# Grouping layer 2's half-array products by two head pairs, C's product as one task, one pool of PSUM banks, and the planner's weight at 25

## The chip, the cores and the metric

The kernel runs on one core of one Trainium2 chip. The metric is the device time of the whole program in microseconds. A ratio is the mean time of one kernel's fast runs over that of the other's fast runs of the same rounds on the same chip, with a 95% interval; it is therefore not quite the ratio of the medians quoted beside it. In the views of the profile PE is TensorE, DVE VectorE, ACT ScalarE and POOL GpSimd, and L605 is line 605 of the kernel.

## The reference, cut to what matters

Four graph layers in a row over 64 graphs of 256 nodes and 512 features, all in fp32. Each layer normalises, applies a relu, and adds its result to x. Layer 2 has 8 heads of 64:

```python
Xp = einsum('bnd,hdk->bhnk', X, Wp) + bp
Xc = einsum('bhnk,hjk->bhnj', Xp, C)
attn = tanh(A[:, None] * einsum('bhnj,bhmj->bhnm', Xc, Xp))
Xh = einsum('bhnm,bhmk->bhnk', attn, Xp)
out = relu(moveaxis(Xh, 1, 2).reshape(B, N, -1))
```

Layer 1 is a masked softmax over neighbours (a leaky relu of a sum of two vectors, plus -1e10 where there is no edge, minus the row maximum, exp).

## The kernel before: the parts concerned

A small planner in Python splits every graph into tasks, keeps five graphs in flight, and emits the tasks in the order in which its own table of engine lengths says they can start. Pools of buffers and PSUM banks are part of that plan; `BEHIND` weighs the older graph against the longer rest of work. The build then still reorders single instructions on each engine.

```python
IN_FLIGHT = 5
BEHIND = 20.0
PAIR_BUFS = 4
ACC_BANKS = 4
# ... (cut)
keep("acc", ACC_BANKS, [P, 512], banks)
keep("tr", 8 - ACC_BANKS, [P, 512], banks)
# ... (cut)  layer 2, one head pair p = heads 2p and 2p+1, each on 64 of the 128 rows
def scores(p):
    @task(f"ps{p}", f"xc{p // 2}", [("PE", 1.1), ("V", 1.37), ("A", 0.7)], {f"pair:th{p}": 1},
          {"xpt": (1, HP), "xc": (1, HP), "at": (1, HP)}, banks=2)
    def _(*ps):
        # ... (cut)
        for m in range(NC):
            for s in range(2):
                half = slice(s * U, (s + 1) * U)
                nc.tensor.matmul(ps[s][:, m, :], g["xpt"][half, p, m * P:(m + 1) * P],
                                 g["xc"][half, p, :], start=True, stop=True)                  # L605
        for s in range(2):
            nc.vector.tensor_tensor(th[:, s], ps[s], g["at"], OP.mult)                        # L608
            nc.scalar.activation(th[:, s], th[:, s], AF.Tanh)                                 # L609
```

`spread(p)` (L626) multiplies the tanh of one pair with Xp, the two heads on two halves of the columns; `times_c` (L589) makes Xc, each head on half the rows and half the columns. The tanh results lie in the same four `pair` buffers as layer 1's attention.

```python
# layer 1, per head pair: ScalarE, then GpSimd, then VectorE, then ScalarE
nc.scalar.activation(e[:, s, j, :], g["all:es"][:, h, :], AF.Prelu, ...)                      # L511, four times
nc.gpsimd.tensor_tensor(e, e, g["negt"][:, None].to_broadcast([P, 2, NC, N]), OP.add)         # L513
nc.vector.tensor_tensor(e, e, g["all:m"][...].to_broadcast([P, 2, NC, N]), OP.subtract)       # L519
nc.scalar.activation(e, e, AF.Exp)                                                            # L521
# and, for the row maxima, on VectorE, 16 times per graph
nc.vector.tensor_tensor_reduce(junk, g["all:en"][:, h, :], g["neg"][:, c, :], ..., OP.max, ...)  # L477
```

## Time and profile before

| | before |
|---|---|
| three runs | 4454.2, 4455.4, 4460.2 us |
| TensorE busy | 98% |
| VectorE, ScalarE, GpSimd busy | 62%, 38%, 26% |

The lines of the page and of the timeline that carry this are in the prediction. First the groups of VectorE: line, operation, tiles and shapes, count, then busy time in total and the mean ns of one, then VectorE's idle time before it and what ended it.

TensorE's waits: who waited for whom, us in total, times, longest.

```profile
PE tr L263 <- DMA mask_rows<-in_nodemask_dram: 25.9, 1, 25.9
PE tr L365 <- DVE hn L357: 12.4, 3, 5.6
...
PE acc L626 <- ACT pair L609: 6.1, 6, 2.9
...
PE tr L440 <- DVE ec L431: 3.4, 2, 3.0
```

The first is the wait for the first loads at the start. The rest is small, and it lies in the first 700 and the last 200 us of the span.

### The profile page before, as it was taken

The numbers are of one execution on the slowest core, as the hardware profiler recorded it, in microseconds if no ns is written. First come the engines' busy times: TensorE is split into PE (matmuls) and PEld (weight loads), VectorE is DVE, ScalarE is ACT, GpSimd is POOL, SyncE is SP. The second block draws the span as 40 slices with busy tenths as digits, with TensorE's granted clock in tenths as the row PEclk, the third lists the DMA queues.
The fourth block names the chain that finished last, engine by engine and source line by source line (L and its number), as shares of the span: only waits on it lengthen the run. The fifth ranks groups of instructions, "written<-read, shape, count | busy, mean of one in ns | idle before, by whom it ended". The sixth has DMA issues, their size and how long they took to land.

```text
span 4449.4 us, 60495 instructions
## 1 busy us (share of the span) xinstructions
PE 4357.1 (98%) x22850; PEld 2997.4 (67%) x22850; DVE 2761.2 (62%) x7530; ACT 1679.7 (38%) x3333; POOL 1175.1 (26%) x969
## 2 busy tenths in 40 slices
PE   6899999999999999999999999999999999999998
PEld 4666666666666667667666666667667666666665
DVE  4765666666666665666666666666666666666653
ACT  1343333433433443443343333333334334334332
POOL 1321222322322322322322222222223223223220
PEclk9899999999999999999999999999999999999999
DMA  4212112122122121221221221221221221221210
GB/s 127 97 54 79 63 70 86 56 79 84 58 79 78 64 79 69 74 79 67 75 77 69 76 77 65 80 77 61 75 86 60 75 86 60 76 86 57 79 53 15
DMA packets 125382, 323.67 MB, mean 73 GB/s; under 512 B 19040, under 2 KB 66208, under 8 KB 100512
## 3 DMA queue, kind: packets, MB, share of 16 engines
q1 hardware_dynamic: 109568, 311.99, 19.3%
q10 hardware_dynamic: 15520, 7.80, 0.7%
q8 instruction: 179, 2.93, 0.3%
q14 instruction: 115, 0.94, 0.1%
HBM read 284.62 MB, written 35.13 MB: 72 GB/s over the span
## 4 chain that ended last, share of the span: by engine, by line
PE 89%; DVE 2%; DMA 1%; issue 0%; ACT 0%; POOL 0%; SPq 0%; POOLq 0%; DVEq 0%; ACTq 0%
PE tr L296 21%; PE acc L296 19%; PE tr L655 10%; PE acc L538 9%; PE tr L605 6%; PE acc L626 6%; PE tr L365 5%; PE tr L681 5%; PE tr L589 3%; PE tr L639 1%; PE tr L574 1%; PE tr L408 1%; DVE junk L477 1%; PE tr L335 1%; PE tr L301 1%
## 5 line engine op out<-in xcount | busy, mean ns | idle before, releaser
L296 PE MATMUL acc<-wv_s,ht 128*128 128x512 f32 x2048 | 932.0, 598 | 1.9 <-ACT ht L366 1.9
L513 POOL TENSOR_TENSOR pair<-pair,negt 128x1024 f32<-128x1024 f32 x256 | 606.7, 2371 | 801.8 <-ACT pair L511 777.1
L609 ACT ACTIVATE pair<-pair 128x512 f32<-128x512 f32 x512 | 310.0, 627 | 884.7 <-DVE pair L608 878.1
L296 PEld LDWEIGHTS acc<-wv_s,ht 128*128 128x128 f32 x2048 | 379.8, 191 | 379.4 <-issue 366.6
L549 POOL TENSOR_TENSOR xt<-xt,o 128x256 f32<-128x256 f32 x256 | 184.5, 731 | 1546.3 <-DVE o L547 1529.3
L538 PE MATMUL acc<-feats,pair 128*128 128x65 f32 x4096 | 508.4, 276 | 10.2 <-DVE xt L316 5.6
L538 PEld LDWEIGHTS acc<-feats,pair 128*128 128x128 f32 x4096 | 491.6, 195 | 37.6 <-issue 25.9
L511 ACT ACTIVATE pair<-all,ec 128x256 f32<-128x256 f32 x1024 | 453.2, 499 | 85.9 <-PE acc L626 50.4
L296 PE MATMUL tr<-w_s,ht 128*128 128x512 f32 x1024 | 465.7, 598 | 2.9 <-ACT ht L366 2.6
L655 PE MATMUL tr<-ht,m_s 128*128 128x256 f32 x2048 | 457.1, 382 | 0.0
L346 DVE BATCH_NORM_STATS2 stats<-xt 128x6 f32<-128x512 f32 x512 | 340.4, 679 | 141.7 <-DMA xt<-in_x_dram 140.7
L655 PEld LDWEIGHTS tr<-ht,m_s 128*128 128x128 f32 x2048 | 386.1, 191 | 54.5 <-issue 4.2
L366 ACT ACTIVATE ht<-tr 128x512 f32<-128x512 f32 x512 | 279.7, 596 | 357.5 <-PE tr L365 297.3
L477 DVE CUSTOM_DVE_ANT_0 junk<-all,neg 128x256 f32<-128x256 f32 x1024 | 390.0, 445 | 4.7 <-DMA all<-er_d 4.6
L357 DVE TENSOR_SCALAR hn<-xt,mv,rstd 128x512 f32<-128x512 f32 x512 | 267.8, 555 | 185.7 <-POOL rstd L351 169.8
L608 DVE TENSOR_TENSOR pair<-tr,at 128x512 f32<-128x512 f32 x512 | 329.3, 683 | 64.2 <-PE tr L605 60.7
L605 PE MATMUL tr<-xc,xpt 64*128 64x256 f32 x2048 | 333.3, 406 | 0.4 <-DVE pair L608 0.4
L521 ACT ACTIVATE pair<-pair 128x1024 f32<-128x1024 f32 x256 | 269.4, 1058 | 166.6 <-DVE pair L519 158.2
L626 PE MATMUL acc<-pair,xp 128*64 128x256 f32 x2048 | 322.0, 396 | 6.2 <-ACT pair L609 6.1
L296 PEld LDWEIGHTS tr<-w_s,ht 128*128 128x128 f32 x1024 | 190.4, 192 | 193.7 <-issue 185.4
L351 POOL TENSOR_TENSOR rstd<-rstd,power 128x2 f32<-128x2 f32 x256 | 227.7, 890 | 313.2 <-DVE rstd L350 296.4
L519 DVE TENSOR_TENSOR pair<-pair,all 128x1024 f32<-128x1024 f32 x256 | 302.6, 1222 | 9.9 <-POOL pair L513 6.3
(87 smaller groups left out, 5272.9 us busy)
## 6 DMA issues: line engine op xcount, KB each, us to landing
all<-er_d SPq DMA_DIRECT2D x128, 1024.0 KB, 4.5
all<-m_d SPq DMA_DIRECT2D x64, 1024.0 KB, 4.6
xt<-in_x_dram SPq DMA_DIRECT2D x64, 512.0 KB, 3.6
adj<-in_adj_dram SPq DMA_DIRECT2D x128, 256.0 KB, 2.6
out_dram<-xt SPq DMA_DIRECT2D x64, 512.0 KB, 4.8
mask_in<-in_nodemask_dram SPq DMA_DIRECT2D x64, 128.0 KB, 3.2
w_n<-in_L_gnn_Wqk_dram ACTq DMA_DIRECT2D x16, 128.0 KB, 3.8
wv_s<-in_L_gnn_W_v_dram ACTq DMA_DIRECT2D x1, 1024.0 KB
```

The lines of the kernel that those rows point to most:

```text
L296: nc.tensor.matmul(p, ht[:, k, c * P:(c + 1) * P], w[:, k], start=(k == 0), stop=(k == KC - 1))
L346: nc.vector.bn_stats(stats[:, c, :], xt[:, c, :])
L477: nc.vector.tensor_tensor_reduce(junk, g["all:en"][:, h, :], g["neg"][:, c, :], 1.0, -BIG, OP.add, OP.max, st["mx"][:, c, h:h + 1])
L511: nc.scalar.activation(e[:, s, j, :], g["all:es"][:, h, :], AF.Prelu, bias=st["ec"][:, j, H + h:H + h + 1], alpha=0.2)
L513: nc.gpsimd.tensor_tensor(e, e, g["negt"][:, None].to_broadcast([P, 2, NC, N]), OP.add)
L519: nc.vector.tensor_tensor(e, e, g["all:m"][:, 2 * p:2 * p + 2, None, :].to_broadcast([P, 2, NC, N]), OP.subtract)
L538: nc.tensor.matmul(po[i][:, h % 4, :], e[:, s, j, i * P:(i + 1) * P], feats[:, j, h, :], start=(j == 0), stop=(j == NC - 1))
L605: nc.tensor.matmul(ps[s][:, m, :], g["xpt"][half, p, m * P:(m + 1) * P], g["xc"][half, p, :], start=True, stop=True)
L608: nc.vector.tensor_tensor(th[:, s], ps[s], g["at"], OP.mult)
L609: nc.scalar.activation(th[:, s], th[:, s], AF.Tanh)
L626: nc.tensor.matmul(pyt[s * U:(s + 1) * U, p % 2, :], g["xp"][:, m, h * U:(h + 1) * U], g[f"pair:th{p}"][:, s, m, :], start=(m == 0), stop= ...
L655: nc.tensor.matmul(pz[:, s, :], m3_s[:, k, d * P:(d + 1) * P], g["ht"][:, k, :], start=(k == 0), stop=(k == KC - 1))
```

## The change

Its intent: let the half-array products of layer 2 stand together in longer groups, so that TensorE changes the shape of its array less often. The two pools of banks become one, and the planner's weight `BEHIND` goes from 20 to 25, which also gives a new order to all the rest. The core of the diff, with cuts marked:

```diff
-BEHIND = 20.0
+BEHIND = 25.0
-ACC_BANKS = 4
+PASSING_BANKS = 4
-    keep("acc", ACC_BANKS, [P, 512], banks)
-    keep("tr", 8 - ACC_BANKS, [P, 512], banks)
+    keep("bank", 8, [P, 512], banks)
 ... (cut: a held bank is granted only if four others are free for passing tasks)
-        def times_c(q):
-            @task(f"xc{q}", ..., [("PE", 1.0), ("V", 0.7)], {} if q else {"xc": 1}, banks=2)
-                        nc.tensor.matmul(pc[s][half, r, :], c2_s[half, 2 * q + r, :],
-                nc.vector.tensor_copy(xc[0:U, 2 * q:2 * q + 2, :], pc[0][0:U])
-                nc.scalar.copy(xc[U:P, 2 * q:2 * q + 2, :], pc[1][U:P])
+        @task("xc", "xpt0 xpt1", [("PE", 1.9), ("V", 0.7)], {"xc": 1}, banks=2)
+                        nc.tensor.matmul(pc[q][half, r, :], c2_s[half, 2 * q + r, :],
+            nc.vector.tensor_copy(xc[:, 0:2, :], pc[0])
+            nc.scalar.copy(xc[:, 2:4, :], pc[1])
-        def scores(p):
-            @task(f"ps{p}", ..., [("PE", 1.1), ("V", 1.37), ("A", 0.7)], {f"pair:th{p}": 1}, ..., banks=2)
+        def scores(q):
+            @task(f"ps{q}", ..., [("PE", 1.95), ("V", 2.75), ("A", 0.7)],
+                  {f"pair:th{2 * q}": 1, f"pair:th{2 * q + 1}": 1}, ..., banks=4)
 ... (cut: spread and its output likewise, two pairs in a task)
```

More of the change, by code (lines that the diff above doesn't have):

```diff
@@ L66, in ready @@
         at = max((ends[d] for d in task.after), default=0.0)
-        need = {"tr": task.banks} if task.banks else {}
+        need = {"bank": task.banks} if task.banks else {}
         for kind, n in task.take.items():
             kind = kind.split(":")[0]
+            if kind == "bank":
+                n += PASSING_BANKS
             need[kind] = need.get(kind, 0) + n
@@ L73, in ready @@
                 return None
-            at = max(at, sorted(self.pools[kind])[n - 1][0])
+            at = max(at, sorted(self.pools[kind])[n - 1 - (PASSING_BANKS if kind == "bank" and not task.banks else 0)][0])
         return at
@@ L84, in issue @@
             g.has.setdefault(kind, []).extend(self.grab(kind.split(":")[0]) for _ in range(n))
-        passing = [self.grab("tr") for _ in range(task.banks)]
+        passing = [self.grab("bank") for _ in range(task.banks)]
         task.run(*[t[2] for t in passing])
@@ L106, in issue @@
             g.until[kind] = max(at, g.until.get(kind, 0.0)) if g.users[kind] else 0.0
-        self.pools["tr"] += [(at, i, t) for _, i, t in passing]
+        self.pools["bank"] += [(at, i, t) for _, i, t in passing]
     def run(self, graph, count):
@@ L205, in passing @@
         turn[0] += 1
-        return plan.pools["tr"][turn[0] % (8 - ACC_BANKS)][2]
+        return plan.pools["bank"][4 + turn[0] % 4][2]
     def load_weight(name, src):
@@ L267, in tile_four_gnn_layers @@
     m3_s = consts.tile([P, KC, D], F32)
-    pm3 = [t for _, _, t in plan.pools["acc"]]
+    pm3 = [t for _, _, t in plan.pools["bank"][:4]]
     wqk3_v = wqk3.rearrange("(k p) (s e) -> p k s e", p=P, s=2)
@@ L374, in _ @@
                 @task(f"pv{layer}{c}", f"ht{layer}{c}" + (f" <pv{layer}0" if c else ""), [("PE", 3.47)],
-                      {"acc": 1}, {"ht": (1, users)})
+                      {"bank": 1}, {"ht": (1, users)})
                 def _():
-                    st[f"pv{c}"] = g.has["acc"][-1][2]
+                    st[f"pv{c}"] = g.has["bank"][-1][2]
                     rows(st[f"pv{c}"], g["ht"], c, wv)
@@ L384, in _ @@
                 st["w"] = softmax_nodes(pr, st["wc"])
-            @task(f"add{layer}", f"soft{layer} pv{layer}0 pv{layer}1", [("V", 1.5)], {}, {"acc": NC})
+            @task(f"add{layer}", f"soft{layer} pv{layer}0 pv{layer}1", [("V", 1.5)], {}, {"bank": NC})
             def _():
@@ L526, in gather @@
             if p % 2:
-                give["acc"] = NC
+                give["bank"] = NC
             @task(f"po{p}", f"eb{p} fb0 fb1" + (f" <po{p - 1}" if p else ""), steps,
-                  {} if p % 2 else {"acc": NC}, give)
+                  {} if p % 2 else {"bank": NC}, give)
             def _():
-                po = [t[2][:, :4 * UE].rearrange("p (q u) -> p q u", q=4) for t in g.has["acc"]]
+                po = [t[2][:, :4 * UE].rearrange("p (q u) -> p q u", q=4) for t in g.has["bank"]]
                 e, feats, xt = g[f"pair:e{p}"], g["feats"], g["xt"]
@@ L577, in graph, with _ @@
             turn_xp(c)
-        def times_c(q):
-            @task(f"xc{q}", "xpt0 xpt1" + (" <xc0" if q else ""), [("PE", 1.0), ("V", 0.7)],
-                  {} if q else {"xc": 1}, banks=2)
-            def _(*pc):
-                pc = [t.rearrange("p (a n) -> p a n", a=2) for t in pc]
-                xpt, xc = g["xpt"], g["xc"]
+        @task("xc", "xpt0 xpt1", [("PE", 1.9), ("V", 0.7)], {"xc": 1}, banks=2)
+        def _(*pc):
+            pc = [t.rearrange("p (a n) -> p a n", a=2) for t in pc]
+            xpt, xc = g["xpt"], g["xc"]
+            for q in range(HP // 2):
                 for r in range(2):
@@ L588, in _ @@
                         half = slice(s * U, (s + 1) * U)
-                        nc.tensor.matmul(pc[s][half, r, :], c2_s[half, 2 * q + r, :],
+                        nc.tensor.matmul(pc[q][half, r, :], c2_s[half, 2 * q + r, :],
                                          xpt[half, 2 * q + r, :], start=True, stop=True)
-                nc.vector.tensor_copy(xc[0:U, 2 * q:2 * q + 2, :], pc[0][0:U])
-                nc.scalar.copy(xc[U:P, 2 * q:2 * q + 2, :], pc[1][U:P])
-        for q in range(HP // 2):
-            times_c(q)
@@ L596, in scores @@
-        def scores(p):
-            @task(f"ps{p}", f"xc{p // 2}", [("PE", 1.1), ("V", 1.37), ("A", 0.7)], {f"pair:th{p}": 1},
-                  {"xpt": (1, HP), "xc": (1, HP), "at": (1, HP)}, banks=2)
+            nc.vector.tensor_copy(xc[:, 0:2, :], pc[0])
+            nc.scalar.copy(xc[:, 2:4, :], pc[1])
+        def scores(q):
+            @task(f"ps{q}", "xc" + (f" <ps{q - 1}" if q else ""), [("PE", 1.95), ("V", 2.75), ("A", 0.7)],
+                  {f"pair:th{2 * q}": 1, f"pair:th{2 * q + 1}": 1},
+                  {"xpt": (1, 2), "xc": (1, 2), "at": (1, 2)}, banks=4)
@@ L599, in _ @@
             def _(*ps):
                 ps = [t.rearrange("p (m n) -> p m n", m=NC) for t in ps]
-                th = g[f"pair:th{p}"]
-                for m in range(NC):
-                    for s in range(2):
-                        half = slice(s * U, (s + 1) * U)
-                        nc.tensor.matmul(ps[s][:, m, :], g["xpt"][half, p, m * P:(m + 1) * P],
-                                         g["xc"][half, p, :], start=True, stop=True)
-                for s in range(2):
-                    nc.vector.tensor_tensor(th[:, s], ps[s], g["at"], OP.mult)
-                    nc.scalar.activation(th[:, s], th[:, s], AF.Tanh)
@@ L612, in spread @@
-        def spread(p):
-            take, give = {} if p % 2 else {"acc": 1}, {f"pair:th{p}": 1, "xp": (1, HP)}
-            if p == 0:
-                take["cols"] = 1
-            if p % 2:
-                give["acc"] = 1
-            @task(f"py{p}", f"ps{p}" + (f" <py{p - 1}" if p else ""),
-                  [("PE", 1.1)] + ([("A", 0.6)] if p % 2 else []), take, give)
-            def _():
-                pyt = g["acc"].rearrange("p (r n) -> p r n", r=2)
-                for m in range(NC):
-                    for s in range(2):
-                        h = 2 * p + s
-                        nc.tensor.matmul(pyt[s * U:(s + 1) * U, p % 2, :], g["xp"][:, m, h * U:(h + 1) * U],
-                                         g[f"pair:th{p}"][:, s, m, :], start=(m == 0), stop=(m == NC - 1))
-                if p % 2:
-                    nc.scalar.activation(g["cols"][:, p - 1:p + 1, :], pyt, AF.Relu)
@@ L630, in graph @@
-        for p in range(HP):
-            scores(p)
-        for p in range(HP):
-            spread(p)
+                for r in range(2):
+                    p = 2 * q + r
+                    for m in range(NC):
+                        for s in range(2):
+                            half = slice(s * U, (s + 1) * U)
+                            nc.tensor.matmul(ps[2 * r + s][:, m, :], g["xpt"][half, p, m * P:(m + 1) * P],
+                                             g["xc"][half, p, :], start=True, stop=True)
@@ new lines, in _, with spread @@
+                for r in range(2):
+                    th = g[f"pair:th{2 * q + r}"]
+                    for s in range(2):
+                        nc.vector.tensor_tensor(th[:, s], ps[2 * r + s], g["at"], OP.mult)
+                        nc.scalar.activation(th[:, s], th[:, s], AF.Tanh)
+        def spread(q):
+            take = {"bank": 1} if q else {"bank": 1, "cols": 1}
+            @task(f"py{q}", f"ps{q}" + (f" <py{q - 1}" if q else ""), [("PE", 1.95), ("A", 0.6)], take,
+                  {f"pair:th{2 * q}": 1, f"pair:th{2 * q + 1}": 1, "bank": 1, "xp": (1, 2)})
+            def _():
+                pyt = g["bank"].rearrange("p (r n) -> p r n", r=2)
+                for r in range(2):
+                    p = 2 * q + r
+                    for m in range(NC):
+                        for s in range(2):
+                            h = 2 * p + s
+                            nc.tensor.matmul(pyt[s * U:(s + 1) * U, r, :], g["xp"][:, m, h * U:(h + 1) * U],
+                                             g[f"pair:th{p}"][:, s, m, :], start=(m == 0), stop=(m == NC - 1))
+                nc.scalar.activation(g["cols"][:, 2 * q:2 * q + 2, :], pyt, AF.Relu)
@@ L635, in back @@
+        for q in range(HP // 2):
+            scores(q)
+        for q in range(HP // 2):
+            spread(q)
         def back(c):
-            @task(f"y{c}", "py1 py3", [("PE", 0.5), ("V", 0.69)], {}, {"cols": (1, NC)}, banks=1)
+            @task(f"y{c}", "py0 py1", [("PE", 0.5), ("V", 0.69)], {}, {"cols": (1, NC)}, banks=1)
             def _(py):
```

## The prediction

> **What bounds the kernel now.** I read the page's busy row first, then the chain of work that ended last, then stretches of the span, then the timeline of TensorE alone.
>
> ```profile
> PE 4357.1 (98%) x22850; PEld 2997.4 (67%) x22850; DVE 2761.2 (62%) x7530; ACT 1679.7 (38%) x3333; POOL 1175.1 (26%) x969
> ...
> PE 89%; DVE 2%; DMA 1%; issue 0%; ACT 0%; POOL 0%; SPq 0%; POOLq 0%; DVEq 0%; ACTq 0%
> ...
> 1000.00:2000.00 1000.00, 1000.00 (x5295) 689.74 (x5294) 630.64 (x1745) 389.55 (x775) 273.11 (x223) 1.00 0.21 74
> 2000.00:3000.00 1000.00, 999.88 (x5292) 689.40 (x5292) 630.17 (x1742) 386.70 (x768) 271.45 (x222) 1.00 0.21 74
> ```
>
> TensorE is busy 98% of the span, 89% of the last chain is TensorE, and in the stretches from 1000 to 3000 us it has no idle time at all (the first busy figure after the stretch's length) at a granted clock of 1.00. The next engine, VectorE, has over a third of its time free. So the time is the length of TensorE's stream, and the 92 us in which TensorE is not busy lie at the two ends: 26 us are the first wait for the weights. A microsecond taken out of the stream is a microsecond of time, unless TensorE then waits.
>
> The second question is whether "busy" hides anything, because ends of matmuls are modelled. So I use starts. Every fp32 matmul is two records. In the timeline each row gives start, length, and the number of records:
>
> ```profile
> 2050.44 1.14 PE L605 MATMUL tr<-xc,xpt 64*128 64x256 f32 x8
> 2051.51 1.08 PE L626 MATMUL acc<-pair,xp 128*64 128x256 f32 x8
> 2052.52 1.09 PE L574 MATMUL tr<-ident,xp 128*128 128x128 f32 x8
> 2053.54 1.14 PE L605 MATMUL tr<-xc,xpt 64*128 64x256 f32 x8
> 2054.61 1.09 PE L626 MATMUL acc<-pair,xp 128*64 128x256 f32 x8
> 2055.62 2.00 PE L538 MATMUL acc<-feats,pair 128*128 128x65 f32 x16
> 2057.55 0.65 PE L626 MATMUL acc<-pair,xp 128*64 128x256 f32 x2
> 2058.13 0.70 PE L605 MATMUL tr<-xc,xpt 64*128 64x256 f32 x2
> 2058.75 1.08 PE L626 MATMUL acc<-pair,xp 128*64 128x256 f32 x6
> ```
>
> L605 (scores, half the rows), L626 (output, half the columns) and L589 (C's product, half of both) work on half the array. Inside such a group the starts of the individual records run 7, 209, 7, 209 ns: one record of each head at the same time, 216 ns per pair of records, the same 216 ns that a full 128x256 record takes on L655. Four matmuls should thus take 4 x 216 = 864 ns. But from the start of L605 to that of L626 there are 1.07 us, and from L626 to L574 1.01 us. The difference sits at the border. Over all borders where the shape of the array changes, the first record after it starts 93 to 100 ns late, and the next one again late: 104 ns late on entering L605, 51 ns on L626 and L589, 70 ns in the mean on coming back to full size (49 after transposes, 104 after 256 columns). A border costs 150 to 200 ns. The last rows show a second loss: a lone matmul (x2) has no partner, and its two records run one after the other, 216 ns apart.
>
> **What the Trainium skill says.** "TensorEngine Tiling (Array Packing)", Tiling Modes, Key Properties: changing the tiling mode drains TensorE. The trace agrees and gives it a size, the 93 to 100 ns above plus the late second record. "TensorE: Matmul & The Clock Gate", Part 3, The mechanism: matmuls on different row groups run at the same time, about 4 ns apart; here it is 7 ns. "Perfetto Trace Analysis", Tensor Engine Instruction: the end of a matmul is an estimate; hence starts. On C's product two statements bear: the tiling page (Gotcha 1, PSUM Pressure) says different row tiles cannot write the same bank at once; "PSUM — Partial Sum Buffer", Terms, Quadrant, says different 32-partition quadrants of one bank may be accessed at once. In this trace L626 writes both heads into one bank on different partitions and still starts 7 ns apart, but with column tiles only. No run here shows row tiles doing so; the kernel before gives L589's two heads different banks.
>
> **The change part by part.** No matmul is added or removed (13362 in both built programs); their order changes. I counted borders and group lengths in the two built programs' order of TensorE; for the kernel before this agrees with the trace kind by kind (188 into L605 from full size, 177 from L605 to L626, and so on).
>
> Borders: 1197 before, 523 after. Entries into L605: 312 before, 131 after; L626: 315 and 105; L589: 129 and 64; back to full size: 441 and 223.
> Before: 1197 x 0.0955 = 114 us, plus 312 x 0.104 = 32, plus 315 x 0.051 = 16, plus 129 x 0.051 = 7, plus 441 x 0.070 = 31: 200 us.
> After: 523 x 0.0955 = 50, plus 14, 5, 3 and 16: 88 us. Saved: 112 us.
>
> Lone matmuls: before, groups are often cut in 1 + 3 (60 groups of one and 56 of three on L605, 62 and 62 on L626), because the first matmul of a group waited for something other than the rest and the build set it apart; the trace has 590 half-array records without a partner, which is 295 matmuls. After, nearly all groups have 8 or 16 matmuls in alternating halves and I count 12 odd groups. A lone matmul costs 432 ns instead of half of 432: 283 x 0.216 = 61 us saved.
>
> Off the path: C's product is copied out once per graph as two full 128x512 halves instead of two times two 64x512 pieces. That removes 64 copies of 0.68 us on VectorE (44 us) and 64 of 0.58 us on ScalarE (37 us). Neither bounds: worth 0.
>
> What it adds: the chain behind a score group gets longer. Before, two multiplications (L608, 0.68 us each) and a tanh (L609, 0.63) stood between scores and output; now four of each. In half of the graphs the built order puts only 8 output matmuls of the first half (8 x 0.216 + 0.2 = 1.9 us) between the second score group and its output. The multiplications start when the group is half done, 0.8 us before its end, so the first tanh pair ends about 1.6 us after it (in time for 1.9) and the second about 2.9 us after it, needed at 2.75 us; in VectorE's order a max of L477 (0.45) stands between the multiplications, and a 0.50 us activation (L511) stands between the tanhs. I expect 0.4 to 0.8 us of waiting in those 32 graphs and a little elsewhere: 25 us, an estimate.
>
> Sum: 4455.4 - 112 - 61 + 25 = 4307 us, or 3.3% less.
>
> **Rivals.** (1) Waits take the place of the borders: score groups need four banks and VectorE for 2.7 us at a stretch. For it: the tight chain above. Against it: waits on this path before are small (6.1 us in total for L626 on L609, 0.4 us for L605 on L608), the one pool has all 8 banks, and in the built order a score bank is used again 2.6 us of TensorE work later at the least, 8.0 us in the median. If every graph lost 1.5 us, 96 us instead of 25, the time would be 4378, within 2%.
> (2) C's product loses its concurrency in the shared bank. Then 512 matmuls take 432 ns instead of 216: +110 us, 4417 us. For it: one sentence of the tiling page; against it: the other page, and L626's 7 ns. I give it 8%.
> (3) All the gain comes and no wait: 4282 us. If also the coming-back cost falls more than I assume, because fewer borders meet 256-column work, 4270.
> (4) VectorE becomes the bound: 2761 - 44 = 2717 us of work in 4300, 63%; it can't be on average, only locally, which is rival 1.
>
> **Range and chances.** The border and pair counts are exact and their costs have a spread of a few ns, so the 173 us are good to 15. The waits, with a new order in the first and last 100 us as well, may be 0 to 70. That gives 4255 to 4360 as the range for 8 in 10. Faster by over 2% means under 4366: 0.86, the rest being rivals 1 and 2. Slower by 2% would need 260 us of new waits: 0.01.
>
> **What would show each step right or wrong.** In the profile after, TensorE should still be at 97 to 98%. Busy time of the three groups should fall: scores from 333 to about 255, output from 322 to about 245, C's product from 141 to about 122. The timeline should show rows of x16 and x32 for them, and records 7 and 209 ns apart inside; a C product at 216 ns per record means rival 2, and its busy time would then exceed 220. VectorE's total should be near 2717 and ScalarE's near 1643. In the table of waits the output group's wait for the tanh should be the largest in the steady part, 15 to 30 us; over 90 us there, or a long wait of the score group for a bank, means rival 1. If borders fall to 523 in the trace and the time does not follow, the costs per border are wrong.

## More of the kernel before

```profile
L477 DVE CUSTOM_DVE_ANT_0 junk<-all,neg 128x256 f32<-128x256 f32 x1024 | 390.0, 445 | 4.7 <-DMA all<-er_d 4.6
...
L519 DVE TENSOR_TENSOR pair<-pair,all 128x1024 f32<-128x1024 f32 x256 | 302.6, 1222 | 9.9 <-POOL pair L513 6.3 <-DMA all<-m_d 3.6
...
L488 DVE TENSOR_SCALAR low<-mx 128x16 f32<-128x16 f32 x64 | 126.5, 1977 | 2.1
```

The maximum L477 and the subtraction L519 are the two large VectorE operations that read two tensors from SBUF. Their means, 445 and 1222 ns, are close to their medians, 422 and 1219. L488 is tiny, has one input from SBUF, and yet takes 1977 ns; what holds it is seen below.

## The result, and the profile after

The changed kernel took 4474.8 us (4470.2 to 4478.2, 4 runs), the kernel before 4454.8 in the same rounds: ratio 1.0044 (1.0026 to 1.0061). The time is the same within 2%, and 168 us over the prediction. The busy row and the chain that ended last:

```profile
PE 4262.3 (95%) x22850; PEld 3001.8 (67%) x22850; DVE 2858.7 (64%) x7466; ACT 1627.7 (36%) x3269; POOL 1203.4 (27%) x969
...
PE 54%; issue 16%; DVE 13%; POOL 4%; DMA 2%; ACT 1%; SPq 0%; POOLq 0%; DVEq 0%; ACTq 0%
```

TensorE's busy time fell by 95 us, but the span did not: TensorE is now busy 95%, and only 54% of the chain is TensorE where it was 89%; VectorE has 13% and GpSimd 4% of it. VectorE is 97 us busier than before although 44 us of copies were taken from it. The three changed groups (lines L604, L625 and L588 stand for L605, L626 and L589 of before):

```profile
L604 PE MATMUL bank<-xc,xpt 64*128 64x256 f32 x2048 | 280.5, 395 | 14.0 <-ACT ex L306 8.2 <-DVE xc L590 5.3 <-ACT cols L627 0.5
L625 PE MATMUL bank<-pair,xp 128*64 128x256 f32 x2048 | 279.9, 389 | 17.0 <-ACT pair L610 17.0
...
L588 PE MATMUL bank<-xpt,c_s 64*64 64x256 f32 x1024 | 124.7, 383 | 0.2 <-ACT xpt L575 0.2
```

Before, they were these:

```profile
L605 PE MATMUL tr<-xc,xpt 64*128 64x256 f32 x2048 | 333.3, 406 | 0.4 <-DVE pair L608 0.4
L626 PE MATMUL acc<-pair,xp 128*64 128x256 f32 x2048 | 322.0, 396 | 6.2 <-ACT pair L609 6.1
...
L589 PE MATMUL tr<-xpt,c_s 64*64 64x256 f32 x1024 | 141.3, 389 | 2.4 <-DVE feats L461 2.4
```

C's product came down to what was predicted, the other two made 68% and 55% of the predicted way. VectorE's groups tell where its time went:

```profile
L477 DVE CUSTOM_DVE_ANT_0 junk<-all,neg 128x256 f32<-128x256 f32 x1024 | 543.5, 581 | 51.2 <-DMA all<-er_d 50.6
L519 DVE TENSOR_TENSOR pair<-pair,all 128x1024 f32<-128x1024 f32 x256 | 399.5, 1574 | 122.0 <-POOL pair L513 115.7 <-DMA all<-m_d 6.3
...
L488 DVE TENSOR_SCALAR low<-mx 128x16 f32<-128x16 f32 x64 | 33.7, 527 | 2.1
```

The same instruction on tiles of the same shape takes 581 instead of 445 ns in the mean, and 1574 instead of 1222. The small L488 went the other way, from 1977 to 527. And VectorE stood idle 115.7 us before L519 for GpSimd's L513, where it was 6.3. TensorE's waits:

```profile
PE bank L296 <- ACT ht L366: 43.6, 62, 3.0
PE bank L440 <- DVE ec L431: 43.0, 29, 1.5
PE bank L263 <- DMA mask_rows<-in_nodemask_dram: 25.4, 1, 25.4
PE bank L574 <- DVE xp L565: 20.7, 31, 0.8
PE bank L492 <- DVE mx L490: 18.2, 3, 9.2
PE bank L625 <- ACT pair L610: 17.0, 39, 3.9
```

The waits for L366, L431, L565 and L490 are nearly new (4.5, 3.4, 2.1 and 1.2 us before). None of them belongs to layer 2's score groups. A period of two graphs repeats every 135 to 137 us, and the same waits come in each. One such place, in the timeline (start, length, engine, line, count; in brackets the idle time before it and what ended it):

```profile
2042.98 2.10 PE L296 MATMUL bank<-w1a_s,ht 128*128 128x272 f32 x8
...
2043.57 4.66 POOL L513 TENSOR_TENSOR pair<-pair,negt 128x1024 f32<-128x1024 f32 x2 [9.62 <-ACT pair L511]
...
2045.96 3.35 DVE L519 TENSOR_TENSOR pair<-pair,all 128x1024 f32<-128x1024 f32 x1 [3.99 <-POOL pair L513]
...
2046.22 3.60 PE L296 MATMUL bank<-w_s,ht 128*128 128x512 f32 x8
...
2049.23 0.16 DVE L431 COPY ec<-bank 128x16 f32<-128x16 f32 x1
...
2049.34 1.06 ACT L521 ACTIVATE pair<-pair 128x1024 f32<-128x1024 f32 x1 [3.78 <-DVE pair L519]
...
2050.31 0.58 ACT L366 ACTIVATE ht<-bank 128x512 f32<-128x512 f32 x1
...
2050.94 2.10 PE L296 MATMUL bank<-w1a_s,ht 128*128 128x272 f32 x8 [1.11 <-ACT ht L366]
...
2053.41 0.68 DVE L565 TENSOR_TENSOR xp<-bank,b_bc 128x512 f32<-128x512 f32 x1
...
2054.15 0.66 PE L574 MATMUL bank<-ident,xp 128*128 128x128 f32 x4 [0.68 <-DVE xp L565]
...
2055.39 1.19 DVE L519 TENSOR_TENSOR pair<-pair,all 128x1024 f32<-128x1024 f32 x1
2056.50 0.17 DVE L431 COPY ec<-bank 128x16 f32<-128x16 f32 x1
...
2056.72 0.28 PE L440 MATMUL bank<-ident,ec 128*16 128x128 f32 x1 [1.48 <-DVE ec L431]
```

Read it from the top. GpSimd adds the mask to two head pairs, one after the other (L513, 4.66 us in all, so about 2.33 each). When the first is done, at about 2045.9, VectorE may subtract the maximum from it: it has waited 3.99 us for this, with all its later work behind it. But just then GpSimd begins the second addition. L519 takes 3.35 us instead of 1.2: it stands still until L513 ends at 2048.2 and needs its own time after that. ScalarE has its exp (L521) next in order and waits 3.78 us for L519; the copy of ht (L366) stands behind the exp, and TensorE's L296 waits 1.11 us for ht. The late VectorE then lets TensorE wait 0.68 us for xp and 1.48 us for ec. So one meeting of two operations on engines that are 64% and 27% busy costs three waits of the engine that sets the time.

I counted this in both traces, taking an instruction to stand beside L513 if L513 covers over 60% of it:

| | L477 beside L513 | mean ns, beside / otherwise | L519 beside L513 | mean ns, beside / otherwise |
|---|---|---|---|---|
| before | 15 of 1024 | 1964 / 423 | 0 of 256 | - / 1222 |
| after | 70 of 1024 | 2453 / 444 | 29 of 256 | 3353 / 1346 |

The multiplication L609, which reads one operand from PSUM, is not slowed: it took 674 ns in 29 cases beside L513 and 681 otherwise; nor are the statistics L346, with one SBUF input, 684 and 676. But the TENSOR_SCALAR operations, also with one SBUF tensor, are: in the kernel before 56 of the 64 L488 stand beside L513 and take 2212 ns, against 166 with no GpSimd work beside (after: 2 of 64), and after the change 32 of the 256 L350 take 1382 ns, against 161. So the kernel before has long meetings too, but at a place where they cost TensorE little: it waits 1.2 us in all for what follows L488 (L492). For the two large operations, that is the rule of "SBUF — State Buffer", Who interferes with whom: a VectorE instruction with two SBUF inputs and a GpSimd instruction that reads SBUF exclude each other, and the second to start blocks until the first is through. The page was there to be read before the prediction; I had looked up only the pages on TensorE, PSUM and the trace.

To see how the whole stream balances, I added up the starts of TensorE's records (from one start to the next) in three parts: the bare passes at 216 ns and the like, lone ones included; what is lost at the borders; and everything else, which is waiting:

| us | before | after | difference | predicted |
|---|---|---|---|---|
| passes | 4115.9 | 4090.4 | -25.5 | -61 |
| borders (1197, then 523) | 213.1 | 102.7 | -110.4 | -112 |
| waiting | 87.3 | 247.9 | +160.6 | +25 |
| sum | 4416.3 | 4441.0 | +24.7 | -148 |

The spans differ by 24.4 us, so the table closes. What it calls waiting is not all idle time. The trace marks stretches of 3.4 us or more in which TensorE's granted clock is 0.5; in them 128x256 records start 427 ns apart instead of 216. They add up to 60.9 us before and 85.4 us after, which costs some 30 and 43 us (an estimate, half of each), so about 12 of the 160.6 us are slow passes and not waits. The gain of the borders came in full. Why the passes gave less is seen here, in the changed kernel's timeline of TensorE:

```profile
2031.06 1.95 PE L625 MATMUL bank<-pair,xp 128*64 128x256 f32 x16
...
2034.17 1.56 PE L604 MATMUL bank<-xc,xpt 64*128 64x256 f32 x10
2036.02 1.13 PE L604 MATMUL bank<-xc,xpt 64*128 64x256 f32 x6 [0.29 <-ACT ex L306]
```

The group of 16 at 2031.06 runs through: 1.88 us to the next start. The score group at 2034.17 is cut after 10 records, because its sixth matmul waits for a bank (ScalarE's L306 has to read it first). The idle time shown is 0.29 us, but from 2034.17 to the next work at 2037.08 there are 2.91 us where an unbroken group needs 8 x 0.216 + 0.104 + 0.09 = 1.92 (the last two are the late records at its two borders). The missing 0.98 us are 0.45 of wait, counted by starts, 0.43 for two lone matmuls (the fifth and the last have lost their partners) and 0.10 for a second late record. At run time there are 354 half-array records without a partner, not the 24 of the built order.

### The profile page after: what moved, and what is told of

It reads as the page before. It is cut to its first block, busy times and chain, and to the rows that moved or that the text cites. A ratio compares the mean times of both kernels' runs of the same rounds, so it can differ in the third digit from the quotient of the medians.

```text
span 4473.8 us, 60529 instructions
## 1 busy us (share of the span) xinstructions
PE 4262.3 (95%) x22850; PEld 3001.8 (67%) x22850; DVE 2858.7 (64%) x7466; ACT 1627.7 (36%) x3269; POOL 1203.4 (27%) x969
## 4 chain that ended last, share of the span: by engine, by line
PE 54%; issue 16%; DVE 13%; POOL 4%; DMA 2%; ACT 1%; SPq 0%; POOLq 0%; DVEq 0%; ACTq 0%
PE bank L296 26%; PE bank L538 8%; PE bank L653 5%; PE bank L365 3%; DVE pair L519 3%; DVE junk L477 3%; PE bank L679 3%; PE bank L588 2%; DMA all<-er_d 2%; PE bank L604 2%; DVE pair L609 2%; POOL pair L513 2%; DVE stats L346 2%; POOL am L670 1%; DVE hn L357 1%
## 5 line engine op out<-in xcount | busy, mean ns | idle before, releaser
L296 PE MATMUL bank<-wv_s,ht 128*128 128x512 f32 x2048 | 921.7, 595 | 0.0
L513 POOL TENSOR_TENSOR pair<-pair,negt 128x1024 f32<-128x1024 f32 x256 | 612.1, 2402 | 859.2 <-ACT pair L511 843.5
L296 PEld LDWEIGHTS bank<-wv_s,ht 128*128 128x128 f32 x2048 | 374.9, 191 | 384.2 <-issue 381.9
L477 DVE CUSTOM_DVE_ANT_0 junk<-all,neg 128x256 f32<-128x256 f32 x1024 | 543.5, 581 | 51.2 <-DMA all<-er_d 50.6
L538 PEld LDWEIGHTS bank<-feats,pair 128*128 128x128 f32 x4096 | 482.0, 192 | 7.0 <-issue 2.1
L538 PE MATMUL bank<-feats,pair 128*128 128x65 f32 x4096 | 485.1, 272 | 0.0
L519 DVE TENSOR_TENSOR pair<-pair,all 128x1024 f32<-128x1024 f32 x256 | 399.5, 1574 | 122.0 <-POOL pair L513 115.7
L296 PE MATMUL bank<-w_s,ht 128*128 128x512 f32 x1024 | 459.3, 596 | 7.5 <-ACT ht L366 7.5
L653 PE MATMUL bank<-ht,m_s 128*128 128x256 f32 x2048 | 461.0, 381 | 0.0
L653 PEld LDWEIGHTS bank<-ht,m_s 128*128 128x128 f32 x2048 | 384.1, 190 | 63.1 <-issue 14.7
L521 ACT ACTIVATE pair<-pair 128x1024 f32<-128x1024 f32 x256 | 270.7, 1057 | 422.9 <-DVE pair L519 408.7
L366 ACT ACTIVATE ht<-bank 128x512 f32<-128x512 f32 x512 | 293.7, 594 | 335.6 <-PE bank L365 335.5
L346 DVE BATCH_NORM_STATS2 stats<-xt 128x6 f32<-128x512 f32 x512 | 336.1, 678 | 109.4 <-DMA xt<-in_x_dram 98.6
L357 DVE TENSOR_SCALAR hn<-xt,mv,rstd 128x512 f32<-128x512 f32 x512 | 260.2, 550 | 149.6 <-POOL rstd L351 138.6
L549 POOL TENSOR_TENSOR xt<-xt,o 128x256 f32<-128x256 f32 x256 | 197.0, 780 | 539.0 <-DVE o L547 527.3
L609 DVE TENSOR_TENSOR pair<-bank,at 128x512 f32<-128x512 f32 x512 | 326.7, 681 | 21.0 <-PE bank L604 20.9
L296 PEld LDWEIGHTS bank<-w_s,ht 128*128 128x128 f32 x1024 | 187.7, 191 | 215.1 <-issue 199.9
L625 PE MATMUL bank<-pair,xp 128*64 128x256 f32 x2048 | 279.9, 389 | 17.0 <-ACT pair L610 17.0
L296 PE MATMUL bank<-w1a_s,ht 128*128 128x272 f32 x1024 | 260.2, 402 | 36.1 <-ACT ht L366 36.1
```

What stands on the lines that cost most here:

```text
L296: nc.tensor.matmul(p, ht[:, k, c * P:(c + 1) * P], w[:, k], start=(k == 0), stop=(k == KC - 1))
L346: nc.vector.bn_stats(stats[:, c, :], xt[:, c, :])
L357: nc.vector.tensor_scalar(g["hn"][:, c, :], g["xt"][:, c, :], st["mv"][:, c, 0:1], st["rstd"][:, c:c + 1], op0=OP.subtract, op1=OP.mult)
L366: nc.scalar.activation(g["ht"][:, :, c * P:(c + 1) * P], pt.rearrange("p (k i) -> p k i", k=KC), AF.Relu)
L519: nc.vector.tensor_tensor(e, e, g["all:m"][:, 2 * p:2 * p + 2, None, :].to_broadcast([P, 2, NC, N]), OP.subtract)
L538: nc.tensor.matmul(po[i][:, h % 4, :], e[:, s, j, i * P:(i + 1) * P], feats[:, j, h, :], start=(j == 0), stop=(j == NC - 1))
```

## The experiments

The theory (P): VectorE's two-input operations stand still beside GpSimd's L513, and what lies behind them in VectorE's and ScalarE's order lets TensorE wait. The first rival (Q): the groups themselves do it, since they take and give back two pair buffers and four banks at once (called G in later expectations). Later rivals: the weight `BEHIND` did it (W), or the single pool of banks (B).

**a_small.** The changed kernel with L513 cut to 8 of 256 columns, a wrong result.

```diff
-                nc.gpsimd.tensor_tensor(e, e, g["negt"][:, None].to_broadcast([P, 2, NC, N]), OP.add)
+                nc.gpsimd.tensor_tensor(e[:, :, :, :8], e[:, :, :, :8],
+                                        g["negt"][:, None, :, :8].to_broadcast([P, 2, NC, 8]), OP.add)
```

> The changed kernel with GpSimd's mask addition (L513) cut to 8 of 256 columns; wrong result on purpose, same order of TensorE but for a few transposes, same 523 borders. Theory P (VectorE's two-input instructions in SBUF stand still while GpSimd's long addition runs, L519 took 3353 ns beside it and 1200 alone, and everything behind them in VectorE's order makes TensorE wait): L519 and L477 go back to about 1200 and 420 ns, TensorE's idle time from 211 us to under 100, time 4270 to 4320. Rival Q (the groups themselves: two pair buffers and four banks taken and given back at once): the waits stay, time over 4430.

Measured: 4312.9 us, ratio 0.9677 (0.9663 to 0.9692), within what P said. VectorE's two groups and TensorE's largest waits of this run:

```profile
L477 DVE CUSTOM_DVE_ANT_0 junk<-all,neg 128x256 f32<-128x256 f32 x1024 | 403.9, 445 | 62.4 <-DMA all<-er_d 61.8
L519 DVE TENSOR_TENSOR pair<-pair,all 128x1024 f32<-128x1024 f32 x256 | 338.1, 1334 | 64.2 <-POOL pair L513 54.5 <-DMA all<-m_d 9.6
```

```profile
PE bank L263 <- DMA mask_rows<-in_nodemask_dram: 25.7, 1, 25.7
PE bank L625 <- ACT pair L610: 15.5, 38, 1.7
PE bank L296 <- ACT ht L366: 11.3, 34, 3.0
```

L477 is back at 445 ns and the waits for ec and xp are gone from the top. L519 stays at 1334, above the 1222 of before: 29 of them still take 2.3 us, because they start while GpSimd's mask product (L670) runs and go on about 1.1 us after its end, the length of a free L519. Waiting fell from 247.9 to some 90 us. Q is out as the main cause: the groups, their buffers and their 523 borders are all still there.

One thing besides the length of L513 differs in this run. The build exchanged a few instructions once in every two graphs: the second L519 now comes ahead of the addition of xp and the two L357, and the copy of ec ahead of the second L357 (VectorE's order differs from the changed kernel's at 551 of 7466 positions, TensorE's and ScalarE's at 58 each). a_split4 and a_split8 below have exactly the order of a_small on these three engines. The exchange stands at the very place of the timeline above, so the waits for ec, 43.0 us in the changed kernel, may have gone with it and not with L513; no run takes it alone. The wait for ht in that timeline comes before the exchanged instructions; the waits for ht fell from 43.6 to 11.3 us.

**b_small.** The control, the same cut in the kernel before.

> The kernel before with the same cut of L513. P: only 15 of its L477 and 2 of its L519 run beside L513, and TensorE has no idle time in the steady part, so the time stays within 0.5% of 4455. If it falls by 2% or more, L513 holds back both kernels and P does not explain the difference. Q says the same as P here.

Measured: 4415.0 us, ratio 0.9907 (0.9892 to 0.9922). That is more than the 0.5% I had allowed: L513 costs the kernel before some 42 us too, against 162 us in the changed one. The order of TensorE is the same here to the last instruction, and the place differs: 35 of the 42 us lie in the first 700, where the graphs in flight fill up, and from TensorE's 3000th record to its 21500th the distance between the two runs stays at 35 us. In the changed kernel it grows from 41 to 159 us over the same records. With the cut in both, the change is worth 4312.9 against 4415.0, 102 us or 2.3%. So L513's presence, with the exchange, takes about 120 us from the change.

**a_split4** and **b_split4.** L513 as four instructions of a quarter each in both kernels, with the right result. It takes away only the length for which VectorE can be held.

```diff
-                nc.gpsimd.tensor_tensor(e, e, g["negt"][:, None].to_broadcast([P, 2, NC, N]), OP.add)
+                for s in range(2):
+                    for j in range(NC):
+                        nc.gpsimd.tensor_tensor(e[:, s, j], e[:, s, j], g["negt"][:, j], OP.add)
```

> The changed kernel with L513 as four instructions of a quarter each, right result. P: VectorE waits for the end of one GpSimd instruction only, about 0.6 us instead of up to 2.15, so L519 stays under 2000 ns and the time falls to 4330 to 4400. Q, or a rival in which the total of GpSimd's work in SBUF is what counts: no change, 4460 to 4490.

> The kernel before with L513 in four quarters: 4445 to 4460, as nothing waits on it. It is the control for the run before it.

Measured: 4379.3 us, ratio 0.9824 (0.9808 to 0.9840), and 4448.9 us, ratio 0.9987 (0.9972 to 1.0002). Both as P said. VectorE's two groups of the changed kernel in quarters (its line numbers are two higher from L515 on), and TensorE's waits:

```profile
L477 DVE CUSTOM_DVE_ANT_0 junk<-all,neg 128x256 f32<-128x256 f32 x1024 | 470.9, 511 | 70.5 <-DMA all<-er_d 70.0
L521 DVE TENSOR_TENSOR pair<-pair,all 128x1024 f32<-128x1024 f32 x256 | 352.3, 1389 | 100.5 <-POOL pair L515 93.3 <-DMA all<-m_d 7.2
```

```profile
PE bank L576 <- DVE xp L567: 28.6, 31, 1.2
...
PE bank L627 <- ACT pair L612: 16.2, 37, 3.2
...
PE bank L296 <- ACT ht L366: 11.3, 33, 3.0
```

The L519 beside L513 take 1737 ns instead of 3353. 95 us of time went, though GpSimd's busy time rose from 1203.4 to 1392.1. The wait for ht fell from 43.6 to 11.3, which shorter standing still explains; the wait for ec is gone too, but may be the exchange's. So by these waits shorter standing still is worth about a third of the 95 us, and how much more isn't shown. What L513 costs in one unchanged order is shown by a_split4 against a_small (66 us), by b_small (42) and by the two cut orders further below (314 and 238). The 93.3 us that VectorE idles for the result of the addition stay: it is in order, and the subtraction is placed before the additions are done.

The control says something more. In the kernel before, the quarters bring more meetings than they take: 212 of its maxima stand beside an addition, at 929 ns, and VectorE spends 540 us on L477 instead of 456. The time does not move. Standing still costs little by itself; it costs where TensorE's next operand is behind it.

**a_split8.** GpSimd's three large operations in pieces of 128 columns (L513 in eight, the mask product L670 in four, the output addition L549 in two per row block; edit as above).

> The changed kernel with GpSimd's three large operations in pieces of 128 columns (L513 in eight, the mask product in four, the output addition in four instead of two), right result. P, with VectorE standing still only to the end of one GpSimd instruction: about 0.3 us per meeting instead of 0.6 in quarters; time 4340 to 4370, under the 4379 of the quarters. If it is the whole length of GpSimd's chain that delays, no gain over the quarters: 4375 or more.

Measured: 4385.8 us, ratio 0.9844 (0.9829 to 0.9858). P's further gain did not come. L477's mean fell to 467 and L519's to 1289 ns, but VectorE's wait for the addition stayed, at 109.9 us, and GpSimd's busy time rose from 1203 to 1671 us, as a piece of 128 columns takes 490 ns in the mean where a quarter took 791. Past quarters, what is left is the length of GpSimd's chain and VectorE's order; that last part is read from the traces, no run takes it away alone.

**b_beh25** and **a_beh20.** Each kernel with the other's `BEHIND`, one number changed.

> The kernel before with only the ordering weight BEHIND at 25 instead of 20. Its built order has 953 borders and 134 odd groups instead of 1197 and 244: at 0.167 us per border and 0.216 us per odd group that is 41 + 24 = 65 us less, 4390, if no new waits come. Theory W (the weight moved VectorE's subtraction L519 beside GpSimd's addition L513, whatever the groups): L519's mean rises from 1222 to about 1570 ns, idle time of TensorE over 180 us, 4450 or more. Theory G (the groups did it): L519 stays near 1220 and the time is 4380 to 4410.

> The changed kernel with only BEHIND back at 20: 528 borders, 68 odd groups; without new waits 112 + 38 = 150 us under before, 4305. W: L519 goes back to about 1220 ns and the time to 4300 to 4350. G: L519 stays over 1500 ns and the time over 4420.

Measured: 4587.7 us, ratio 1.0299 (1.0284 to 1.0315), and 4752.6 us, ratio 1.0666 (1.0641 to 1.0691). Neither W nor G has it as they were worded: the kernel before gets slow at 25, as W said, but the changed one much slower at 20, where W said 4300 to 4350; and there L519 is at 1221 ns, where G said over 1500. a_beh20's largest waits are these:

```profile
PE bank L365 <- DVE hn L357: 129.8, 30, 4.8
PE bank L408 <- DVE qk L398: 105.9, 25, 4.2
PE bank L335 <- DVE o L547: 35.1, 26, 4.4
```

The waits stand at other places than at 25. L357, which makes hn, is one more TENSOR_SCALAR that stands still: 681 ns in the mean here, 543 in a_beh20_small below, where L513 is cut and the order the same. So P is too narrow in naming two-input operations alone. In that run 110 of the L477 stand beside L513, at 2247 ns in the mean, and none of the L519. In b_beh25 it is 77 and 18.

**a_2pools20.** The groups and C's product, but the two pools and `BEHIND` 20 of the kernel before.

> The groups and C's product in one bank, but the two pools of four banks and BEHIND 20 of the kernel before: 612 borders, 42 odd groups; without new waits 98 + 44 = 142 us less, 4313. If the one pool is what shifted the order (theory B), this one has L519 near 1220 ns and is under 4350; under G it has L519 over 1500 ns or other new waits over 100 us, and is over 4400.

Measured: 4965.1 us, ratio 1.1148 (1.1132 to 1.1165), the slowest of all. B falls. The cause of most of it is plain and a different one (L624 is the output, L609 the tanh):

```profile
PE acc L624 <- ACT pair L609: 322.5, 59, 6.0
```

The outputs stand right behind the scores and wait for the tanh; 46 of these waits lie in the stretch from 700 to 4200 us, 5.8 us each in the mean. I take it that the planner finds nothing to put between them, as one score group takes all four passing banks. a_beh20 differs from this run only in having one pool of eight, and waits 6.8 us in all there. So this is the wait that the prediction feared, and at `BEHIND` 20 the single pool is what avoids it.

**b_xc.** The kernel before with only C's product changed.

> The kernel before with C's product alone changed to one task with both heads in a bank: 920 borders, 110 odd groups, so 46 + 29 = 75 us less, 4380, if it keeps its concurrency (records 7 ns apart) and no new waits come. If its order brings L513 beside L519, L519's mean is over 1400 ns and the time 4420 or more.

Measured: 4790.2 us, ratio 1.0759 (1.0743 to 1.0775). The product itself was as expected (pairs 7 ns apart in one bank), but the new order brought 67 of the L477 beside L513 and waits of the scores for the copy of Xc (59.5 us).

**a_beh20_small** and **b_xc_small.** The two slow orders again with L513 cut to 8 columns; TensorE's and ScalarE's orders are unchanged to the last instruction, and VectorE's differs at 7 and 35 of 7466 positions. The counts in what was expected of them take any GpSimd work beside L477, hence 76 where the count above has 67, and slightly other means.

> The changed kernel with BEHIND 20 (4752.6 us) and L513 cut to 8 columns, wrong result on purpose; TensorE's order is the same. P: its 110 maxima L477 beside L513, of 2195 ns in the mean, go back to under 1000, and the time falls by 300 us or more, to 4300 to 4420. If P holds only for the changed kernel at 25 and this order is bad for another reason, it stays over 4600.

> The kernel before with C's product changed alone (4790.2 us) and L513 cut to 8 columns, wrong result on purpose; TensorE's order is the same. P: the 76 maxima of 1980 ns go, and the time falls to 4360 to 4450, 75 us under the 4415 of the kernel before with the same cut being the best it can do. If the product's own waits are the cause (the scores wait for the copy of C's product, L602 on L590), it stays over 4600.

Measured: 4438.1 us and 4551.9 us. The cut takes 314 us from a_beh20 and 238 us from b_xc. Against the kernel before the two orders lose 299 and 336 us, so L513's presence is most of it, but both end above the range given: waits of the ordinary kind remain (82.7 us for hn in the first, 62.8 in the second). So L513's presence explains most of what these orders lose, not all of it; the cut takes away the standing still and the length of GpSimd's chain at once.

**a_port.** The changed kernel with a fifth resource in the planner that layer 1's slopes, subtractions and maxima must hold in turn:

```diff
+            if engine in "VG" and task.name.startswith(("ea", "eb", "max")):
+                start = max(start, self.free["S"])
+                self.free["S"] = start + length
```

> The changed kernel with one more resource in its planner, which the slopes on GpSimd and the maxima and subtractions on VectorE must hold in turn, so that the order it builds keeps L513 from standing beside L477 and L519. 646 borders and 76 odd groups: 92 + 36 = 128 us under before, 4327, without waits. P: L519 near 1220 and L477 near 430 ns, time 4330 to 4400. If the planner's times are too far from the chip's, the meetings come back elsewhere and the time is anywhere up to 4800; then it tells only that an order cannot be trusted before it has run.

Measured: 4582.0 us, ratio 1.0286 (1.0269 to 1.0303). The meetings did come back elsewhere: 49 of L477 and 13 of L519. I take it that the planner's table is too far from the chip's times for such a rule to hold. This one failed.

All runs side by side, by time. "Held" is an estimate of the time that VectorE stands still: over all its instructions with over 60% of their length beside L513 or its pieces, and over 1.3 times plus 50 ns as long as the median of the same instruction with no GpSimd work beside, what they take beyond that median. The clock is the mean granted one of TensorE.

| run | us | ratio | borders | L477 / L519 beside L513 | held, us | clock |
|---|---|---|---|---|---|---|
| a_small (wrong result) | 4312.9 | 0.968 | 523 | 3 / 0 | 0 | 0.998 |
| a_split4 | 4379.3 | 0.982 | 523 | 173 / 29, quarters | 112 | 0.994 |
| a_split8 | 4385.8 | 0.984 | 523 | 183 / 29, eighths | 65 | 0.992 |
| b_small (wrong result) | 4415.0 | 0.991 | 1197 | 3 / 0 | 0 | 0.995 |
| a_beh20_small (wrong result) | 4438.1 | 0.996 | 528 | 11 / 0 | 0 | 0.986 |
| b_split4 | 4448.9 | 0.999 | 1197 | 212 / 0, quarters | 177 | 0.992 |
| before | 4454.8 | 1 | 1197 | 15 / 0 | 156 | 0.993 |
| after | 4474.8 | 1.004 | 523 | 70 / 29 | 260 | 0.990 |
| b_xc_small (wrong result) | 4551.9 | 1.022 | 920 | 12 / 0 | 0 | 0.988 |
| a_port | 4582.0 | 1.029 | 646 | 49 / 13 | 229 | 0.976 |
| b_beh25 | 4587.7 | 1.030 | 953 | 77 / 18 | 250 | 0.988 |
| a_beh20 | 4752.6 | 1.067 | 528 | 110 / 0 | 413 | 0.955 |
| b_xc | 4790.2 | 1.076 | 920 | 67 / 0 | 323 | 0.964 |
| a_2pools20 | 4965.1 | 1.115 | 612 | 122 / 1 | 378 | 0.941 |

The number of borders does not order this table. Of the orders with the full L513, the kernel before has the fewest meetings of L477 and L519 and the least held time, and most of that is L488's.

A part of the slow orders' loss is the clock, not waiting. In the stretches at half clock passes take twice as long, so span times (1 - clock) estimates their cost: 214 us in a_beh20, 172 in b_xc and 293 in a_2pools20, against 31 in the kernel before. That is about half of what these three lose. With L513 cut and TensorE's order unchanged it falls to 62 us (a_beh20_small) and 55 (b_xc_small), so it came with what L513 brings. That the waits bring it is likely, but no run separates the two.

I take it that the weight of 20 of the kernel before had been found by trying, as the changed kernel's 25 must have been; no run shows that.

## Why the prediction was wrong

The range was 4255 to 4360, the time 4474.8.

- What bounds the kernel: right for the kernel before. "A microsecond taken out of the stream is a microsecond of time, unless TensorE then waits": the second half came true.
- Borders: 523 as counted, 102.7 us for the predicted 88. The difference to before, 110.4 us, is the predicted 112.
- C's product in one bank: right. Its busy time is 124.7 us (about 122 predicted), its records start 7 ns apart, and the 8% rival is out.
- Lone matmuls: right in kind, mis-sized. I took the built order for what happens, 12 odd groups. A wait inside a group breaks its pairs, so 177 matmuls stayed alone and the gain was 25.5 us instead of 61.
- Off the path: ScalarE fell to 1627.7 us (1643 predicted). VectorE was to fall to 2717 and rose to 2858.7. "Neither bounds: worth 0" was true of the removed copies, but the step assumed that a VectorE instruction keeps its length in a new order. L477, L519 and L350 did not.
- What it adds: this is the step that failed. "I expect 0.4 to 0.8 us of waiting in those 32 graphs and a little elsewhere: 25 us." The wait of the outputs for the tanh was sized right, 17.0 us. The "little elsewhere" was the rest of +160.6 us of waiting. I had worked out only the chain that the change touches, while a new order moves every chain against every other. The run with L513 cut shows that the addition's presence accounts for 162 us of the changed kernel's time (with the exchange of a few instructions that the cut brought) and 42 us of the kernel before's.
- One reading is too wide, without bearing on the sum: "every fp32 matmul is two records" isn't so for transposes, which leave one (13362 instructions, 22850 records).
- Rival 1 had the right direction and the wrong reason and size (96 us at the most, in the score groups). Rival 4 said VectorE can be a bound "only locally, which is rival 1"; locally it was, but in layer 1.

Not settled: how the last 66 us between quarters (4379) and almost no addition (4313) divide into short meetings and VectorE's waiting in order for GpSimd's result; how much of the 95 us of the quarters the exchanged instructions brought; and why the grouped order places the subtraction where it does, since every other order tried had meetings of its own.

The fastest version with the right result is the changed kernel with L513 in quarters, 1.8% under the kernel before (the one in eighths, 1.6%, overlaps it within the intervals); the quarters alone give the kernel before 0.1%, within the noise.

## What to carry to other kernels

In a kernel whose instruction order is planned, a change to one part is a change to the whole order, so predict from what the other engines will stand beside, not only from the chain that was edited. Look for pairs of VectorE operations with two SBUF inputs, or TENSOR_SCALAR ones however small, and large GpSimd operations on SBUF: if they may meet ahead of something TensorE needs, try the GpSimd one in pieces (quarters of 0.79 us went with a gain of 95 us here, eighths of 0.49 us brought no more). And a wait in the middle of a group of paired half-array matmuls can cost several times what shows as idle (0.98 for 0.29 us in the place shown).

## What the Trainium skill lacked or had wrong

- "TensorEngine Tiling (Array Packing)", Tiling Modes: it names the drain at a change of mode but no size. Here the first record comes 93 to 100 ns late and the second again 49 to 104 ns; 1197 changes took 213.1 us.
- The same page, Gotcha 1: that different row tiles cannot write one bank at the same time is too wide. C's product writes two row tiles into one bank, on different partitions, with starts 7 ns apart, and its busy time fell from 141.3 to 124.7 us.
- No page has that a wait inside a group of paired tiles breaks the pairs behind it: 0.29 us of idle time cost 0.98 us.
- "SBUF — State Buffer" has the rule that mattered, and the runs agree (3353 ns for L519 beside L513, 1222 in the kernel before). It names no custom operation; the two-input maximum L477 is subject to it as well (2453 ns beside, 444 otherwise). And it says nothing of what the blocking does to a planned order: with `BEHIND` alone changed the time moved by 3 to 6%, and in the slower of these two orders the addition's presence is worth 314 us.
